# GNN layer with normalisation: 29 node ranges summed from one-hot products and 1610 nodes from row gathers, instead of 35 ranges and 650 nodes

## The chip, the cores and the metric

One core of one Trainium2 chip runs the kernel. The metric is device time of one execution in microseconds. The kernel before took 628.18 us (median of 3 runs, 627.49 to 630.49). Its five engines are TensorE (PE, with its weight loads shown apart as PEld), VectorE (DVE), ScalarE (ACT), GpSimd (POOL) and SyncE (SP); SP only issues transfers here.

## What is computed

There are 6250 nodes with 128 features, and 100,000 edges sorted by destination. An edge of type 0 carries its source's features times W_data plus b_data, an edge of type 1 those times W_control plus b_control. Messages are summed per destination; the node's own product is added, then ReLU, a residual and a layer norm.

```python
m_data = Xs @ W_data.T + b_data          # Xs = X[src]
m_ctrl = Xs @ W_control.T + b_control
msg = jnp.where((edge_types == 0)[:, None], m_data, m_ctrl)
agg = jax.ops.segment_sum(msg, dst, num_segments=X.shape[0])
out = jax.nn.relu(agg + (X @ W_self.T + b_self))
x = _layernorm(x + out, axis=-1)
```

## The kernel before, in words

**The message table.** L422 to L472 compute both products for every node, 128 nodes to a block, two blocks to a round q (25 rounds). Each float32 product is kept as three bfloat16 parts that add up to it (m3, 98 tiles of 128 rows and 384 columns). m3 stays in SBUF and is also written to DRAM as `table`, one transfer per round, on SP for even and on ACT for odd rounds (L470).

**Ranges (windows).** The first 5600 nodes are summed in 35 ranges of WN = 160 nodes, in groups of 1, 2 and eight times 4 ranges (GROUPS, L35). A range reads 2688 sorted edges. `ranks` (L582) works on a group at once. For each of 21 edge columns it builds a one-hot of the source tile (hots, L638), and PE counts with triangular weights how many earlier edges have the same tile (L648, accumulator rk). DVE takes the maximum (slot, L652). Each edge so gets one of 32 slots in its tile. One-hots of the slots (hr, L667; two, L673) scatter the edge's row and destination into those slots (L682). Edges that find no slot go to a list of 64 (hl, L749); their rows are fetched from `table` by a slot gather on POOL (sr, L790), whose index `at` comes from DVE (L778), and copied by SP to gl (L797). The slot table goes through DRAM (packed) and comes back broadcast to all partitions (rows, L832); DVE turns it into one-hots (L840).

`sums` (L823) then runs over the ranges. In each of 25 steps g, PE selects message rows with four matmuls of 32 output rows (L860), ACT or DVE copies the result out of PSUM (gs, L405 or L406), and PE adds it to the destination rows with one-hots hot2 built by DVE (L847): L874 for 128 of the range's nodes, L877 for the other 32.

**The last nodes.** The last 650 nodes are summed in six blocks of up to 128 (`gathered`, L892). A block takes nt columns of 128 edges (GT: 18 for a full block, 3 for the last; 93 in all). DVE works out each edge's table row and its destination code (eight operations of nt columns, L903 to L916). For each column POOL gathers 128 rows of `table` (L924, buffer t_msg, eight of them), DVE builds a one-hot (L929, buffer t_hot), and PE adds (L935) into the single accumulator ga.

**Closes.** `close` (L485) finishes a group of ranges or a block: ACT copies one third of the accumulator and DVE adds the other two (L520, L523), then residual and ReLU (L531), statistics (L535, L537), eight small operations, the scaling on ACT or DVE, and a store by SP (L574). The 32 remaining nodes of a group's ranges are gathered in one further block (f).

**The order of the work.** Every operation is given to `Plan` (L83) with an engine, a duration in us, a due time and what it reads and writes. `Plan.run` (L120) simulates the engines, picks the operation with the earliest due time among those that are ready, and emits the program in that order. Each engine then executes its own list strictly in order. The constants SEM (a hop between engines), OTHER and LAT are part of this model. `add` takes a buffer's ring length (bufs): a buffer is free for reuse when the users of the one that many places before it are through.

Ranges fall due at T0 + 13 us each, and gathers are spread over g0 = T0 + 2 TW to g1 = T0 + (NW - 2) TW (L965 to L970).

Of the kernel before, what the change touches and what calls it, by code (L numbers as in the profile page):

```python
# [33 lines left out]
WIN = KT * P  # L34
GROUPS = [1, 2] + [4] * 8  # L35
NW = sum(GROUPS)
# [7 lines left out]
NGB = -(-(N - NW * WN) // P)  # L44
GT = [-(-(min(P, N - NW * WN - P * i) * 17) // P) + 1 for i in range(NGB)]
NBD = -(-(NW + NGB) // 16) * 16

# [35 lines left out]
class Plan:  # L83
    SEM = 0.12
    OTHER = 0.5
# [34 lines left out]
    def run(self):  # L120
# [31 lines left out]
        while len(order) < n:  # L152
# [75 lines left out]
def act(cols):  # L228
    return 0.055 + cols / 1200

def sums_over_windows(ctx, tc, x, xt, edges, w, bias, out, total):
# [20 lines left out]
    TW = 13.0  # L252
    LAT = 0.15

# [124 lines left out]
    def load_edges(b, n, out_, due, buf, key, engine):  # L379
        def fn():  # L380
# [41 lines left out]
    for q in range(NS):  # L422
# [36 lines left out]
        for i in range(3 if q >= DQ else 0):  # L459
            d = due + 0.6 + 1.2 * i  # L460
            evict(lambda mv3=mv3, i=i: mv3(i), pv3, n, d, [mp], [(m3, (q, i))])
            if i < 2:
# [22 lines left out]
    def close(tag, n0, step, rows, sums_a, block, due):  # L485
# [12 lines left out]
        if block:  # L498
            xb = B(work, [D, len(block), W4], F32, "xb", 2, 4 * W4)
            for j, (at, _) in enumerate(block):  # L500
# [12 lines left out]
            add("PE", 0.6, mms, due, [xb, w_sb, one3, brows, fold] + [b for _, b in block], [f])  # L513
        mv = B(work, [P, nb, 2], F32, "mv" + tag, 2, 10)
        for k in range(nb):
            if k < nw:
                a, da = sums_a[k]
                m = m0
                s = B(work, [P, D], F32, "s", 3)
                add("ACT", act(D), lambda a=a, s=s, m=m: A.copy(s.t[:m], a.t[:m, 0:D]), da, [a],  # L520
                    [s])
                for c in (1, 2):
                    vec(da, D, lambda a=a, s=s, c=c, m=m: V.tensor_add(  # L523
                        s.t[:m], s.t[:m], a.t[:m, c * D : (c + 1) * D]), [a, s], [s])
# [6 lines left out]
            vec(da, D, lambda src=src, k=k, m=m: V.scalar_tensor_tensor(  # L531
                h.t[:m, k, :], src(), 0.0, xr.t[:m, k, :], op0=ALU.max, op1=ALU.add),
                [got] + [(xr, key) for key in keys], [(h, ("a", k))] + [(h, key) for key in keys])
            st = B(work, [P, 6], F32, "st", 4)
            add("DVE", 0.2, lambda k=k, st=st, m=m: V.bn_stats(st.t[:m], h.t[:m, k, :]), da + 1,  # L535
                [(h, ("a", k))], [st])
# [45 lines left out]
    def ranks(gi, w0, nw, when, step, engines):  # L582
# [308 lines left out]

    def gathered(bi, when, step):  # L892
        nt, n0 = GT[bi], NW * WN + bi * P
        nn = min(P, N - n0)
        gi = len(GROUPS) + bi
        top = max(GT)
        G2 = lambda name, dt=F32: B(work, [P, nt], dt, "t_" + name, 2, top)
        raw = B(work, [P, nt, 3], I32, "t_raw", 2, 3 * top)
        load_edges(NW + bi, nt * P, lambda: raw.t, when - 12, raw, None, "SP")
        rel, lows, ins, far, code = (G2(k) for k in ("rel", "lows", "ins", "far", "code"))  # L900
        cb, idx = G2("cb", I32), G2("idx", I32)
        d = when - 6
        vec(d, nt, lambda: V.tensor_scalar_add(rel.t, raw.t[:, :, 1], 1.0 - n0), [raw], [rel])  # L903
        vec(d, nt, lambda: V.tensor_single_scalar(lows.t, rel.t, nn + 0.5, op=ALU.is_lt), [rel],
            [lows])
        vec(d, nt, lambda: V.scalar_tensor_tensor(
            ins.t, rel.t, 0.5, lows.t, op0=ALU.is_ge, op1=ALU.mult,
            accum_out=counts.t[:, gi : gi + 1]), [rel, lows], [ins, (counts, gi)])
        vec(d, nt, lambda: V.tensor_single_scalar(cb.t, raw.t[:, :, 0], 7,
                                                  op=ALU.arith_shift_right), [raw], [cb])  # L910
        vec(d, nt, lambda: V.tensor_single_scalar(far.t, raw.t[:, :, 2], 0.0, op=ALU.not_equal),
            [raw], [far])
        vec(d, nt, lambda: V.tensor_add(far.t, far.t, cb.t), [far, cb], [far])
        vec(d, nt, lambda: V.scalar_tensor_tensor(
            idx.t, far.t, 128.0, raw.t[:, :, 0], op0=ALU.mult, op1=ALU.add), [far, raw], [idx])
        vec(d, nt, lambda: V.tensor_mul(code.t, rel.t, ins.t), [rel, ins], [code])  # L916
        xc = B(work, [D, P], F32, "t_xc", 2)
        add("SP", 0.1, lambda: S.dma_start(xc.t[:, :nn], xt[:, n0 : n0 + nn]), when, m3_key(6), [xc],
            lat=2.5)
        ga = B(ps, [P, 512], F32, "ga", 1)  # L920
        for k in range(nt):
            at = when + step * k
            m = B(work, [P, D3], BF16, "t_msg", 8)
            add("POOL", 1.25, lambda m=m, k=k: G.indirect_dma_start(  # L924
                out=m.t, out_offset=None, in_=table[:, :],
                in_offset=bass.IndirectOffsetOnAxis(ap=idx.t[:, k : k + 1], axis=0)),
                at, [idx, table_b], [m], lat=2.0)
            hot = B(work, [P, P], BF16, "t_hot", 4)
            vec(at + 2, P, lambda hot=hot, k=k: V.tensor_scalar(  # L929
                hot.t, iota1_b.t[:, :P], code.t[:, k : k + 1], None, op0=ALU.is_equal),  # L930
                [code, (iota1_b, 0)], [hot], 0.26)

            def mm(m=m, hot=hot, k=k):
                for j in range(-(-nn // R)):
                    T.matmul(ga.t[R * j : R * j + R, :D3], hot.t[:, R * j : R * j + R], m.t,  # L935
                             start=k == 0, stop=False, skip_group_check=True)
            add("PE", 0.165, mm, at + 4.5, [hot, m], [ga])
        end = when + step * nt + 6
        add("PE", 0.3, lambda: own(lambda j, m: ga.t[R * j : R * j + m, :D],
                                   lambda j, m: xc.t[:, R * j : R * j + m], nn), end,  # L940
            [xc, w_sb, one3, brows], [ga])
        close("g", n0, nn, nn, [(ga, end)], [], end + 2)

# [15 lines left out]
    for gi, w0, nw, *_ in todo:  # L959
# [4 lines left out]
              T0 + (w0 + nw) * TW + 2)  # L964
    total_tiles = sum(GT)  # L965
    g0, g1 = T0 + 2 * TW, T0 + (NW - 2) * TW
    done = 0
    for bi, nt in enumerate(GT):
        gathered(bi, g0 + (g1 - g0) * done / total_tiles, (g1 - g0) / max(total_tiles, 20))
        done += nt  # L970
    total_ps = low()
# [147 lines left out]
```

## Time and profile before

| quantity | value |
|---|---|
| median of 3 runs | 628.18 us |
| the profiled execution, its own time | 627.98 us |
| its span, first to last instruction | 626.0 us |
| mean granted TensorE clock | 0.960 |
| ACT copies of gs, L405 | 835, 353.9 us busy |
| PE selection, L860 | 3430 matmuls |
| gathers by POOL, L924 | 93 |
| slot gathers by POOL, L790 | 18 |
| mean DMA rate | 108 GB/s |

Busy times are unions of the records of an engine. Matmul and DVE records overlap their successors, so the sum of single durations is more than the busy time. The profile's list of groups gives the mean length of one record.

### The profile page before, as it was taken

What the parts mean: (1) busy time and instruction counts of PE and PEld (TensorE: products, weight loads), DVE (VectorE), ACT (ScalarE), POOL (GpSimd) and SP (SyncE); (2) the same over time, 40 slices, a digit from 0 to 9 for tenths busy, and PEclk for the clock granted to TensorE, in tenths of its full rate; (3) what the DMA queues carried; (4) which work ended last, traced back from release to release, by engine and by line L of the source; (5) the groups of instructions that cost most, each with busy time, mean ns of one, the idle gap of its engine ahead of it and who ended that gap; (6) DMA issues with size and microseconds to landing.
All of it is one profiled execution on the core that took longest, in us unless ns stands there. A gap on an engine that the chain in (4) does not pass through costs nothing.

```text
span 626.0 us, 31669 instructions
## 1 busy us (share of the span) xinstructions
PE 547.3 (87%) x13418; PEld 417.8 (67%) x13418; DVE 519.5 (83%) x1848; ACT 447.4 (71%) x1152; POOL 114.0 (18%) x119
## 2 busy tenths in 40 slices
PE   4987979979998899899889998999899899988890
PEld 3554646747776677777667876787677678766670
DVE  6966788999999899998999999899979888865512
ACT  3656656747687767877777788778678777887890
POOL 1000162030411054200134210163100342000000
PEclk9989897979999899999999999999999999998996
DMA  3889372062225313530344143225410442142000
GB/s 89 251 264 278 97 212 88 11 214 67 77 71 176 96 51 109 175 115 5 129 132 143 44 129 115 92 64 161 133 62 7 154 136 83 46 143 76 7 5 26
DMA packets 58585, 67.86 MB, mean 108 GB/s; under 512 B 19390, under 2 KB 49587, under 8 KB 58435
## 3 DMA queue, kind: packets, MB, share of 16 engines
q1 hardware_dynamic: 45585, 48.25, 24.7%
q0 software_dynamic: 5360, 10.98, 6.5%
q10 hardware_dynamic: 7490, 6.52, 3.2%
q8 instruction: 107, 1.75, 1.1%
q14 instruction: 43, 0.35, 0.2%
HBM read 50.73 MB, written 13.27 MB: 102 GB/s over the span
## 4 chain that ended last, share of the span: by engine, by line
DVE 53%; PE 31%; DMA 6%; ACT 4%; issue 3%; SPq 1%; ACTq 0%; DVEq 0%
DVE hot L847 10%; PE a L874 9%; PE g L860 9%; DVE slot L652 8%; PE rk L648 4%; DVE hots L638 4%; DVE two L673 4%; DVE rows L840 3%; ACT gs L405 3%; DVE s L523 3%; PE g L440 2%; DMA rows<-packed 2%; DVE st L535 2%; PE a L877 2%; DVE hr L667 2%
## 5 line engine op out<-in xcount | busy, mean ns | idle before, releaser
L405 ACT CAST gs<-g 128x384 bf16<-128x384 f32 x835 | 353.9, 481 | 98.1 <-PE g L860 90.8
L860 PE MATMUL g<-m,rows 128*32 128x384 bf16 x3430 | 321.0, 332 | 2.4 <-DVE rows L840 1.5
L874 PE MATMUL a<-gs,hot 128*32 128x384 bf16 x3360 | 309.5, 333 | 12.1 <-ACT gs L405 5.3
L860 PEld LDWEIGHTS <-rows 128*32 128x32 bf16 x3430 | 217.7, 135 | 15.1 <-DVE rows L840 2.6
L877 PE MATMUL a<-gs,hot 128*32 128x128 bf16 x2520 | 201.6, 221 | 0.1
L874 PEld LDWEIGHTS <-hot 128*32 128x32 bf16 x3500 | 153.7, 95 | 68.1 <-issue 33.2
L924 POOL DMA_INDIRECT t_msg<-table,t_idx x93 | 94.4, 1015 | 218.5 <-PE ga L935 166.9
L652 DVE TENSOR_REDUCE slot<-rk 128x4 f32<-128x392 f32 (+2 forms) x210 | 106.8, 509 | 17.6 <-PE rk L648 16.1
L847 DVE TENSOR_TENSOR hot<-iota_b,to_d 128x800 bf16<-128x800 bf16 x175 | 94.5, 567 | 25.7 <-PE a L877 20.3
L877 PEld LDWEIGHTS <-hot 128*32 128x32 bf16 x2625 | 98.1, 97 | 5.9 <-issue 0.6
L648 PE MATMUL rk<-hots,rest 128*32 128x392 bf16 (+2 forms) x800 | 74.9, 323 | 25.4 <-DVE slot L652 25.1
L648 PE MATMUL rk<-hots,tri 128*32 128x392 bf16 (+2 forms) x840 | 84.2, 319 | 7.4 <-DVE hots L638 7.4
L648 PEld LDWEIGHTS <-rest 128*32 128x32 bf16 x800 | 35.2, 97 | 48.0 <-issue 43.4
L638 DVE TENSOR_TENSOR hots<-iota_b,st 128x392 bf16<-128x392 bf16 (+2 forms) x210 | 60.5, 330 | 1.3 <-PE vt L682 1.1
L790 POOL DMA_INDIRECT sr<-table,at x18 | 17.0, 943 | 207.1 <-DVE at L778 140.3
L840 DVE TENSOR_SCALAR rows<-rows,pid 128x1568 bf16<-128x1568 bf16 x70 | 42.5, 627 | 4.6 <-DMA rows<-packed 4.5
L648 PEld LDWEIGHTS <-tri 128*32 128x32 bf16 x840 | 36.3, 98 | 11.2 <-DVE tri L312 6.7
L935 PE MATMUL ga<-t_msg,t_hot 128*32 128x384 bf16 x363 | 37.1, 327 | 3.3 <-DVE s L523 2.6
L440 PE MATMUL g<-w_sb,xc 128*128 128x256 f32 x98 | 34.1, 440 | 1.2 <-ACT m L405 0.6
L523 DVE TENSOR_TENSOR s<-s,a 128x128 f32<-128x128 f32 x70 | 19.8, 283 | 16.5 <-ACT s L520 15.4
L405 ACT CAST m<-g 128x512 bf16<-128x512 f32 (+1 forms) x43 | 23.3, 579 | 13.6 <-PE g L465 5.8
L682 PEld LDWEIGHTS <-two 128*64 128x64 bf16 x735 | 18.8, 109 | 15.0 <-DVE two L673 11.3
(173 smaller groups left out, 573.6 us busy)
## 6 DMA issues: line engine op xcount, KB each, us to landing
rows<-packed SPq DMA_DIRECT2D x35, 784.0 KB
table<-m SPq DMA_DIRECT2D x12, 384.0 KB
table<-m ACTq DMA_DIRECT2D x12, 384.0 KB
xc<-in_xt SPq DMA_DIRECT2D x8, 320.0 KB
xr<-in_x SPq DMA_DIRECT2D x8, 256.0 KB
out<-xr SPq DMA_DIRECT2D x8, 256.0 KB
gl<-sr SPq DMA_DIRECT2D x35, 48.0 KB
xc<-in_xt ACTq DMA_DIRECT2D x6, 256.0 KB
```

The lines of the kernel that those rows point to most:

```text
L405: [("ACT", act(cols), lambda: A.copy(o(), src())), ("DVE", dve(cols), lambda: V.tensor_copy(o(), src()))], None, None, due, r, w, lat)
L440: T.matmul(o, xa.t[:, at : at + P], w_sb.t[:, : 2 * D], start=i == 0, stop=False, skip_group_check=True)
L523: vec(da, D, lambda a=a, s=s, c=c, m=m: V.tensor_add(s.t[:m], s.t[:m], a.t[:m, c * D : (c + 1) * D]), [a, s], [s])
L638: vec(due - (2.0 if k else 0.5), nw * NT, lambda k=k, hot=hot, k0=k0: V.tensor_tensor(hot.t[:, k - k0].rearrange("p w (c d) -> p w c d", d=2),
L648: T.matmul(acc.t[R * j : R * j + R, : nw * NT], wt.t[:, R * j : R * j + R], m, start=start, stop=stop, skip_group_check=True)
L652: vec(due, nw * NT, lambda k=k: V.tensor_reduce(slot.t[:, k, :], acc.t[:, : nw * NT].rearrange("p (w c) -> p w c", c=NT), axis=AX.X, op=AL ...
L840: add("DVE", dve(half * NT, 0.26), lambda sp=sp, rs=rs: V.tensor_scalar(sp.t[:, rs], sp.t[:, rs], pid1.t, None, op0=ALU.is_equal), due - 4 ...
L847: V.tensor_tensor(hot2.t[:, c0 : c0 + 5].rearrange("p g (c d) -> p g c d", d=2), iota1_b.t.rearrange("p (c d) -> p c d", d=2)[:, None].to_ ...
L860: T.matmul(gp.t[R * t : R * t + R, :D3], sp.t[:, :, 4 * g + t], m3.t[:, 4 * g + t, :], start=True, stop=True)
L874: T.matmul(a.t[R * j : R * j + R, :D3], hot2.t[:, g, R * j : R * j + R], gs.t, start=g == 0, stop=False, skip_group_check=True)
L877: T.matmul(a.t[R * c : R * c + R, D3:], hot2.t[:, g, P:], gs.t[:, c * D : (c + 1) * D], start=False, stop=last, skip_group_check=True)
L924: add("POOL", 1.25, lambda m=m, k=k: G.indirect_dma_start(out=m.t, out_offset=None, in_=table[:, :], in_offset=bass.IndirectOffsetOnAxis(a ...
```

## The change

The ranges become 29 (groups of 1, 2, six times 4, and 2) and cover 4640 nodes. The last 1610 nodes go to 13 blocks: twelve of 18 columns and one of 11, 227 gathers.

`gathered` now takes up to four blocks at once: one set of the eight preparing operations for all of them, with the blocks' first nodes from gbase. The destination codes are kept in pairs of bfloat16. One DVE operation builds the one-hots of up to six columns (KB) by comparing two tensors. There are six message buffers instead of eight, two one-hot buffers of six columns instead of four of one.

Besides, in `close`, one reduce over the three thirds replaces ACT's copy and two adds; the remainder's xt loads become one transfer. Rounds q with q % 5 of 3 or 4 take their product accumulator from the ring "a" (two) instead of "g" (three). The table goes out in pairs of rounds, on SP alone; the loads of xt go on SP except chunk 1. The copies to to_d are for ACT only. The planner's hop depends on the engine, LAT is 0.1, and some durations are longer.

```diff
-GROUPS = [1, 2] + [4] * 8
+GROUPS = [1, 2] + [4] * 6 + [2]
+GB = 4
-    SEM = 0.12
+    HOP = {"PE": 0.22, "ACT": 0.15, "DVE": 0.11, "POOL": 0.12, "SP": 0.12}
-                    o.ready = max(o.ready, op.end + (0.0 if same else op.lat + self.SEM))
+                    o.ready = max(o.ready, op.end + (0.0 if same else op.lat + self.HOP[e]))
-    LAT = 0.15
+    LAT = 0.1
+    vec(2, 1, lambda: V.memset(counts.t, 0.0), [], [counts])
+    acopy = lambda o, src, cols, due, r, w: add(
+        "ACT", 0.1 + cols / 1000, lambda: A.copy(o(), src()), due, r, w)
-            e = ("ACT", A) if c % 2 else ("SP", S)
+            e = ("ACT", A) if c == 1 else ("SP", S)
-                xa.t, xt[:, c * CH * P : c * CH * P + n]), due - 4, [], [xa], lat=3.0)
+                xa.t, xt[:, c * CH * P : c * CH * P + n]), due - 5, [], [xa], lat=3.0)
-        mp = B(ps, [P, 512], F32, "g", 3)
+        mp = B(ps, [P, 512], F32, *(("a", 2) if q % 5 > 2 else ("g", 3)))
-        e = ("ACT", A) if q % 2 else ("SP", S)
-        add(e[0], 0.1, lambda ts=ts, e=e: e[1].dma_start(tv[:, ts, :], m3.t[:, ts, :]), due + 8,
-            m3_key(q), [(table_b, q)], lat=3.5)
+        if q % 2 or q == NS - 1:
+            t0 = 4 * (q - q % 2)
+            add("SP", 0.1, lambda t0=t0, t1=ts.stop: S.dma_start(
+                tv[:, t0:t1, :], m3.t[:, t0:t1, :]), due + 8, m3_key(q) + m3_key(q - q % 2),
+                [(table_b, q)], lat=4.5)
-                add("SP", 0.1, lambda at=at, j=j: S.dma_start(
-                    xb.t[:, j, :], xt[:, at : at + R]), due - 20, late, [(xb, j)], lat=2.5)
+            add("SP", 0.1, lambda: S.dma_start(
+                xb.t, xt[:, b0:b1_].rearrange("d (b p) -> d b p", p=WN)[:, :, P:]), due - 20, late,
+                [xb], lat=2.5)
-                add("ACT", act(D), lambda a=a, s=s, m=m: A.copy(s.t[:m], a.t[:m, 0:D]), da, [a],
-                    [s])
-                for c in (1, 2):
-                    vec(da, D, lambda a=a, s=s, c=c, m=m: V.tensor_add(
-                        s.t[:m], s.t[:m], a.t[:m, c * D : (c + 1) * D]), [a, s], [s])
+                vec(da, D3 + 70, lambda a=a, s=s, m=m: V.tensor_reduce(
+                    s.t[:m], a.t[:m, :D3].rearrange("p (c d) -> p d c", c=3), axis=AX.X,
+                    op=ALU.add), [a], [s])
-                copy(lambda t=t, par=par, nx=nx: to_d.t[R * t : R * t + R, par : nw : 2, :nx, :],
+                acopy(lambda t=t, par=par, nx=nx: to_d.t[R * t : R * t + R, par : nw : 2, :nx, :],
+    gbase = C([P, NGB], I32, "gbase")
+    add("POOL", 0.2, lambda: G.iota(gbase.t, pattern=[[P, NGB]], base=NW * WN - 1,
+                                    channel_multiplier=0), 3, w=[gbase])
+    def gathered(bis, when, step):
+        nt, k_ = GT[bis[0]], len(bis)
+        n = nt * k_
+        raw = B(work, [P, k_, nt, 3], I32, "t_raw", 2, 3 * top)
+        for j, bi in enumerate(bis):
+            load_edges(NW + bi, nt * P, lambda j=j: raw.t[:, j], when - 14 + 0.1 * j, raw, j, "SP")
+        G2 = lambda name, dt=F32: B(work, [P, k_, nt], dt, "t_" + name, 1, top)
+        cb, idx = G2("cb", I32), B(work, [P, n], I32, "t_idx", 2, top)
+        code = B(work, [P, n, 2], BF16, "t_code", 2, 2 * top)
...
+        vec(d, 2 * n, lambda: V.tensor_tensor(code.t, f2(rel), f2(ins), op=ALU.mult), [rel, ins],
+            [code])
+        KB = 6
+        for j, bi in enumerate(bis):
...
+            start = when + step * nt * j
...
+            ga = B(ps, [P, 512], F32, "ga", 1)
+            for k in range(nt):
+                at = start + step * k
+                kk = j * nt + k
+                if k % KB == 0:
+                    kn = min(KB, nt - k)
+                    hot = B(work, [P, kn, P], BF16, "t_hot", 2, KB * P)
+                    s4 = [P, kn, P // 2, 2]
+                    vec(at + 1, kn * P, lambda hot=hot, kk=kk, kn=kn, s4=s4: V.tensor_tensor(
+                        hot.t.rearrange("p k (c d) -> p k c d", d=2),
+                        iota1_b.t[:, :P].rearrange("p (c d) -> p c d", d=2)[:, None]
+                        .to_broadcast(s4), code.t[:, kk : kk + kn, None, :].to_broadcast(s4),
+                        op=ALU.is_equal), [code, (iota1_b, 0)], [hot], 0.52)
+                m = B(work, [P, D3], BF16, "t_msg", 6)
+                add("POOL", 1.25, lambda m=m, kk=kk: G.indirect_dma_start(
+                    out=m.t, out_offset=None, in_=table[:, :],
+                    in_offset=bass.IndirectOffsetOnAxis(ap=idx.t[:, kk : kk + 1], axis=0)),
+                    at, [idx, table_b], [m], lat=2.0)
...
+            close("g", n0, nn, nn, [(ga, end)], [], end + 2)
+    step = max((g1 - g0) / max(sum(GT), 20), 1.3)
+    full = len(GT) - (GT[-1] != GT[0])
+    for b0 in range(0, NGB, GB):
+        for bis in (range(b0, min(b0 + GB, full)), range(max(b0, full), min(b0 + GB, NGB))):
+            if len(bis):
+                gathered(list(bis), g0 + step * done, step)
```

More of the change, by code (lines that the diff above doesn't have):

```diff
@@ L499, in close @@
             xb = B(work, [D, len(block), W4], F32, "xb", 2, 4 * W4)
+            b0, b1_ = block[0][0] - P, block[-1][0] + R
             for j, (at, _) in enumerate(block):
@@ L530, in close @@
                 got, src = f, lambda f=f, m=m: f.t[:m, :D]
-            vec(da, D, lambda src=src, k=k, m=m: V.scalar_tensor_tensor(
+            vec(da, D + 70, lambda src=src, k=k, m=m: V.scalar_tensor_tensor(
                 h.t[:m, k, :], src(), 0.0, xr.t[:m, k, :], op0=ALU.max, op1=ALU.add),
@@ L534, in close @@
             st = B(work, [P, 6], F32, "st", 4)
-            add("DVE", 0.2, lambda k=k, st=st, m=m: V.bn_stats(st.t[:m], h.t[:m, k, :]), da + 1,
+            add("DVE", 0.28, lambda k=k, st=st, m=m: V.bn_stats(st.t[:m], h.t[:m, k, :]), da + 1,
                 [(h, ("a", k))], [st])
@@ L889, in sums @@
         return got
[L892 to L904, printed above, removed]
+    gbase = C([P, NGB], I32, "gbase")
@@ new lines, in sums_over_windows @@
+    add("POOL", 0.2, lambda: G.iota(gbase.t, pattern=[[P, NGB]], base=NW * WN - 1,
[3 more added lines that the diff above has]
+        n = nt * k_
+        gi = len(GROUPS) + bis[0]
+        top = GB * max(GT)
+        raw = B(work, [P, k_, nt, 3], I32, "t_raw", 2, 3 * top)
+        for j, bi in enumerate(bis):
+            load_edges(NW + bi, nt * P, lambda j=j: raw.t[:, j], when - 14 + 0.1 * j, raw, j, "SP")
+        G2 = lambda name, dt=F32: B(work, [P, k_, nt], dt, "t_" + name, 1, top)
+        rel, lows, ins, far = (G2(k) for k in ("rel", "lows", "ins", "far"))
+        cb, idx = G2("cb", I32), B(work, [P, n], I32, "t_idx", 2, top)
+        code = B(work, [P, n, 2], BF16, "t_code", 2, 2 * top)
+        d = when - 8
+        nn = min(P, N - NW * WN - P * bis[0])
+        fl = lambda b: b.t.rearrange("p b k -> p (b k)")
+        f2 = lambda b: fl(b)[:, :, None].to_broadcast([P, n, 2])
+        vec(d, n, lambda: V.tensor_sub(
+            rel.t, raw.t[:, :, :, 1], gbase.t[:, bis[0] : bis[0] + k_, None].to_broadcast(
+                [P, k_, nt])), [raw, gbase], [rel])
+        vec(d, n, lambda: V.tensor_single_scalar(lows.t, rel.t, nn + 0.5, op=ALU.is_lt), [rel],
@@ L905, in gathered @@
             [lows])
-        vec(d, nt, lambda: V.scalar_tensor_tensor(
+        vec(d, n, lambda: V.scalar_tensor_tensor(
             ins.t, rel.t, 0.5, lows.t, op0=ALU.is_ge, op1=ALU.mult,
             accum_out=counts.t[:, gi : gi + 1]), [rel, lows], [ins, (counts, gi)])
[L909 to L942, printed above, removed]
+        vec(d, n, lambda: V.tensor_single_scalar(cb.t, raw.t[:, :, :, 0], 7,
+                                                 op=ALU.arith_shift_right), [raw], [cb])
+        vec(d, n, lambda: V.tensor_single_scalar(far.t, raw.t[:, :, :, 2], 0.0,
+                                                 op=ALU.not_equal), [raw], [far])
@@ new lines, in gathered, with mm @@
+        vec(d, n, lambda: V.tensor_add(far.t, far.t, cb.t), [far, cb], [far])
+        vec(d, n, lambda: V.scalar_tensor_tensor(
+            idx.t.rearrange("p (b k) -> p b k", k=nt), far.t, 128.0, raw.t[:, :, :, 0],
+            op0=ALU.mult, op1=ALU.add), [far, raw], [idx])
+        vec(d, 2 * n, lambda: V.tensor_tensor(code.t, f2(rel), f2(ins), op=ALU.mult), [rel, ins],
+            [code])
+        KB = 6
+        for j, bi in enumerate(bis):
+            n0 = NW * WN + bi * P
+            xc = B(work, [D, P], F32, "t_xc", 2)
+            start = when + step * nt * j
+            add("SP", 0.1, lambda xc=xc, n0=n0: S.dma_start(xc.t[:, :nn], xt[:, n0 : n0 + nn]),
+                start, m3_key(6), [xc], lat=2.5)
+            ga = B(ps, [P, 512], F32, "ga", 1)
[16 more added lines that the diff above has]
+                    at, [idx, table_b], [m], lat=2.0)
+                def mm(m=m, hot=hot, k=k, ga=ga):
+                    for i in range(-(-nn // R)):
+                        T.matmul(ga.t[R * i : R * i + R, :D3], hot.t[:, k % KB, R * i : R * i + R],
+                                 m.t, start=k == 0, stop=False, skip_group_check=True)
+                add("PE", 0.165, mm, at + 4.5, [hot, m], [ga])
+            end = start + step * nt + 6
+            add("PE", 0.3, lambda ga=ga, xc=xc: own(
+                lambda i, m: ga.t[R * i : R * i + m, :D],
+                lambda i, m: xc.t[:, R * i : R * i + m], nn), end, [xc, w_sb, one3, brows], [ga])
+            close("g", n0, nn, nn, [(ga, end)], [], end + 2)
@@ L964, in sums_over_windows @@
               T0 + (w0 + nw) * TW + 2)
-    total_tiles = sum(GT)
     g0, g1 = T0 + 2 * TW, T0 + (NW - 2) * TW
+    step = max((g1 - g0) / max(sum(GT), 20), 1.3)
     done = 0
-    for bi, nt in enumerate(GT):
-        gathered(bi, g0 + (g1 - g0) * done / total_tiles, (g1 - g0) / max(total_tiles, 20))
-        done += nt
+    full = len(GT) - (GT[-1] != GT[0])
[3 more added lines that the diff above has]
+                gathered(list(bis), g0 + step * done, step)
+                done += sum(GT[bi] for bi in bis)
     total_ps = low()
```

## The prediction, made before the result was known

> **What bounds the kernel now.** I read the busy shares first, then stretches of 60 us in the steady part, then the pace of TensorE (PE) where it runs alone, then GpSimd (POOL), whose work the change grows most. The page's first part:
>
> ```profile
> PE 547.3 (87%) x13418; PEld 417.8 (67%) x13418; DVE 519.5 (83%) x1848; ACT 447.4 (71%) x1152; POOL 114.0 (18%) x119
> ```
>
> PE and VectorE (DVE) share the work; POOL is idle four fifths of the time. Two stretches, each as long as one group of four ranges (columns: stretch, length, busy of PE, PEld, DVE, ACT, POOL, granted clock, DMA share, GB/s):
>
> ```profile
> 247.00:307.00 60.00, 54.91 (x1496) 43.88 (x1500) 55.18 (x188) 46.14 (x120) 5.70 (x6) 1.00 0.31 95
> 307.00:367.00 60.00, 55.18 (x1496) 44.15 (x1488) 56.01 (x192) 46.00 (x121) 19.65 (x20) 1.00 0.37 114
> ```
>
> Both engines are 92 to 93% busy, so neither has slack: a group costs about 60 us because it needs 55 us on each of two coupled engines. The second stretch holds 18 gathers' matmuls (72 by the tile ga), the first 4 (16), and the time is the same within what the stretches show. The list step L749, once per group, starts at 130.96, 184.99, 246.87, 305.20, 366.67, 426.32, 484.54 and 543.8: periods of 54 to 62 us. After the last, PE and ACT work off about six ranges until 609 us, and the last close and store take 17 us more. The pace of PE alone, from the timeline near the end (start, length):
>
> ```profile
> 554.77 0.35 PE L874 MATMUL a<-gs,hot 128*32 128x384 bf16 x4
> 554.93 0.24 PE L877 MATMUL a<-gs,hot 128*32 128x128 bf16 x3
> 554.96 0.38 PE L860 MATMUL g<-m,rows 128*32 128x384 bf16 x4
> 555.16 0.35 PE L874 MATMUL a<-gs,hot 128*32 128x384 bf16 x4
> ```
>
> One step of a range (L860, L874, L877) repeats every 0.39 us, though the records last 0.35 each: they overlap. Four matmuls of 384 columns are 1536 of the step's 3456 columns, 0.173 us. A row's mean is therefore not its cost; the spacing is. POOL:
>
> ```profile
> 82.24 0.95 POOL L924 DMA_INDIRECT t_msg<-table,t_idx  x1 [0.30 <-issue]
> 83.49 0.94 POOL L924 DMA_INDIRECT t_msg<-table,t_idx  x1 [0.30 <-issue]
> ...
> L924 POOL DMA_INDIRECT t_msg<-table,t_idx x93: 940/946/1753, 77.2 to 521.1; - x93
> ...
> POOL t_msg L924 <- PE ga L935: 166.9, 39, 31.7
> POOL sr L790 <- DVE at L778: 140.3, 9, 39.3
> ```
>
> Gathers follow each other every 1.25 us when nothing holds them (mean busy 1.015 + 0.30 = 1.31). POOL otherwise waits for free message buffers or, in order, for the slot gather sr.
>
> **Part by part: PE.** One range of 160 nodes costs 25 steps x 0.39 + 0.28 (own product, L479 and L482 at 551.64) = 10.0 us. A four-range group adds its rank passes: 41 passes of 392 columns x 0.177 = 7.2, the slot scatter 2.6 (L682 in 307 to 367), prefix and lists 0.9, its remainder block 0.5: 11.2 us. Two such groups go: 2 x (40.0 + 11.2) = 102.4. One two-range group comes: 20.0 + 41 x 0.09 (spacing at 196 columns near 62.5 us) + 1.3 + 0.9 + 0.3 = 26.2. Added: 134 gathers x 0.173 = 23.2, and 7 own products of closes x 0.28 = 2.0. Net -51.0 us of PE. At the 92% of the stretches, -55: span 626.0 - 55 = 571.
>
> **DVE.** In 307 to 367, with each line's own busy time: L847 10.98, L840 4.94, L652 11.49, L638 6.49, L667 2.00, L673 3.70, L523 2.84, L929 4.01. Of the 56.0 I take off L929 and one gathered close with its preparation (about 4) and have 48 us for a four-range group. Two go (-96). The two-range group: L638 21 x 0.19, L652 21 x 0.27, one-hots of slots 3.3, L847 and L840 8.0, closes 2.5, small operations about 7: +30.5. Seven more gathered closes, each one reduce 0.55, L531 0.22, L535 0.22, L537 0.11, eight small ones at 0.15, one scale 0.2 = 2.5: +17.5. The gather one-hots: 93 x 0.22 (4.01/18) = 20.7 become 38 of up to 768 columns at the 0.52 of the nearest row (L673 at 768, 0.552 less overlap): 19.7, -1. Preparation: six times 1.32 (43.18 to 44.50) becomes four times about 1.7, -1. The to_d copies on DVE (37 x 0.15) move to ScalarE (ACT), -6. Net -56; over 0.925, -61: span 565.
>
> **One reduce for a copy and two adds.** Nearest row: L652, 392 columns out of PSUM, 0.559, against 2 x 0.283 for L523. Taken as nothing; the strided read is not in the trace, and at half rate it would be 42 x 0.41 = +17 us, which I keep for the range. ACT loses 42 copies of 0.27.
>
> **ACT** loses 150 evictions at 0.42 (five in 2.1 near 75 us), 63 us, against 37 copies x 0.27 = 10 gained: it stays off the bound.
>
> **A third sum, by periods.** L749 of the first four-range group stays at 131. Then five periods: the first 54 to 58, four with about 33 gathers instead of 6 to 20. Periods with 20 gathers issued took 62, those with 6 took 58 and 59: 0.25 us per gather, so about 65. That gives 131 + 58 + 260 = 449. The two-range group's period: 2.5 ranges worked off meanwhile, 37, to 486. Then 5.5 ranges remain (six less 2.5, plus two): 56, some last gathers 3, the end 17: 562. The three sums say 571, 565, 562; I take 566. Around the span lie 627.98 - 626.0 = 2.0 us, hence 568; the profiled execution is 0.2 below the median of 628.18, which I leave.
>
> **POOL.** 227 gathers and 15 slot gathers (18 less the two for each of two groups, plus one) x 1.31 = 317 us, between 76 us (L790 and the first gather, when the table is complete) and about 525: 70% of it. It is covered while six message buffers (eight before) are enough: PE takes one each 1.9 us (430/227), so six cover 11.4 us. The Trainium skill speaks against this part: "SBUF — State Buffer", section "A bandwidth-pool intuition that's wrong (but worth ruling out)", says that a DMA whose descriptors GpSimd writes took about 3.1 us instead of 0.62 beside a VectorE copy holding the port they share. By the rule 242 x 3.1 = 750 us, more than the span. The row decides: median 946 and longest 1753 ns with DVE 92% busy, so 317 us.
>
> Landing: the chain of waits has
>
> ```profile
> 188.04 5.09 DMA sr<-table,at
> ```
>
> while "DMA: Bandwidth & Descriptors", section "Anatomy of one DMA — SWDGE (gpsimd) path", fits 2.0 us plus bytes over 436 GB/s, 2.2 us for 98 KB, about what the planner books. By the fit a buffer is held 2.2 us before PE can use it, by the row 5.1 (the gather's 0.95 within it); I take the row, leaving 11.4 - 5.1 = 6 us of cover.
>
> **Queues and waits that move.** SP takes all table writes (13 instead of 25 in all) and five more loads of xt; it drops 3 issues per block (0.42 each) and gains 7 edge loads (0.83) and three issues for each of 7 closes (0.5), about 16 us over 450. The closes' stores wait on SP for DVE; behind them stand loads of rows, which are issued 12 planned us ahead. Cover gone, each costs up to 2 us: 14. In the head the table writes now wait on one queue behind and ahead of range loads; SP waited there 14.5 us for ACT's m, and DVE 4.3 for rows. Five banks for the products instead of three work against that. Together -6 to +8; taken 0, since the end of the table is set by 25 rounds on ACT. The new durations in the planner only reorder; the idle of PE, 4.7 in 60, bounds a gain at about 25 us, and I allow as much loss; taken 0. The memset and the iota (0.15) lie before 2 us.
>
> **Rivals.** *Dry buffers at the slot gathers:* POOL stops at sr until DVE has at; the gathers behind it are stuck, and PE stands before a message with its ranges queued behind. For it: 140.3 us in nine waits. Against: those stood where no gather was due. Price: eight groups' waits, each one landing less one step, 5.1 - 1.9 = 3.2 us, 26 us: about 594. *Slower:* turnaround of the six buffers becomes the bound. PE frees a buffer late because its fixed order puts other work between, POOL refills late, PE waits. It decides when one turn of six exceeds 6 x (626 - 76 - 30)/227 = 13.7 us; at 15 us (2.5 each) 76 + 568 + 30 + 2 = 676. Against it: ten gathers passed in 13 us from 411 to 424, though with eight buffers. *The better order:* half of PE's idle goes, about 552.
>
> **How the numbers follow.** The sums hold 0.58 (556 to 580), dry buffers 0.20 (580 to 610), better order 0.09 (544 to 556), slower 0.11, and 0.02 lands within 0.5%, about what a measurement of this kernel can tell from no change, by both losses at once. Faster 0.87, same 0.02, slower 0.11. The range 546 to 606 leaves out the slow rival, some of the far ends, about 2 in 10.
>
> **What would show it.** Right: PE about 496 and DVE about 463 us busy, POOL 240 to 250; nothing or little under PE waiting for t_msg; L749 periods of 63 to 67; spacing 1.25 at L924. Wrong: PE waiting for DMA t_msg for more than 20 us; L924 busy over 1.5 us; the strided reduce near 1 us; the table complete after 82 us.

## The result and the profile after

The kernel after takes 548.13 us (median of 4 runs, 547.09 to 550.25) beside 627.84 us for the kernel before (4 runs, 626.32 to 630.49): a ratio of 0.873, with a 95% interval of 0.869 to 0.877. The forecast was 568 us, with a range of 546 to 606: the time lies in it, near its lower end. 80 us went where 60 were forecast. Lines move by a few: L860 is now L866, L874 L880, L877 L883, L652 L658, L749 L755, L790 L796, L924 L958, L935 L965, L929 L952.

The page's first part, for the kernel after (span 546.8 us, own time 548.72 us):

```profile
PE 483.3 (88%) x11972; PEld 380.5 (70%) x11972; DVE 463.3 (85%) x1615; ACT 387.0 (71%) x981; POOL 252.2 (46%) x251
```

DVE lost 56 us of busy time and PE 64, and POOL's more than doubled. Two stretches of one four-range group each (columns as before):

```profile
249.00:313.00 64.00, 59.15 (x1614) 48.05 (x1606) 60.61 (x201) 47.42 (x122) 38.61 (x39) 1.00 0.49 141
313.00:375.00 62.00, 58.49 (x1597) 48.85 (x1592) 58.18 (x183) 48.07 (x126) 38.37 (x39) 1.00 0.49 144
```

A group now carries 36 gathers and takes 62 to 64 us. PE and DVE are 92 to 95% busy in it: the same two engines bound the kernel, a little more tightly than before. The waits (engine, tile and line, releaser: us in total, times, longest; dots stand for rows left out):

```profile
POOL t_msg L958 <- PE ga L965: 93.6, 78, 21.8
...
POOL t_msg L958 <- PE g L866: 41.0, 68, 2.4
...
POOL sr L796 <- DVE at L784: 13.9, 7, 7.2
...
PE rk L654 <- DVE slot L658: 8.4, 17, 1.3
...
PE a L880 <- ACT gs L407: 5.5, 10, 1.2
```

POOL waits for PE to free message buffers. For the slot gathers' index it waits hardly any more (13.9 us against 140.3; one wait of 65.8 us in the head, before the table is complete, stays as it was, 64.4 before). PE has no wait for t_msg at all. The tile t_msg, and two of the by-form groups of VectorE (busy, mean ns | idle before):

```profile
L958 POOL DMA_INDIRECT t_msg<-table,t_idx x227: 940/947/2712, 78.8 to 505.3; - x114
```

```profile
L952 DVE TENSOR_TENSOR t_hot<-iota_b,t_code 128x768 bf16<-128x768 bf16 x37 | 20.5, 553 | 1.4 <-PE ga L965 1.3
L528 DVE TENSOR_REDUCE s<-a 128x128 f32<-128x384 f32 x29 | 16.0, 553 | 24.8 <-ACT bs L407 15.2
```

A gather occupies POOL for 0.947 us in the median (0.946 before), the first starts at 78.8 us instead of 77.2, and the one reduce takes 0.553 us, about as much as the two adds of 0.283 that it replaces; ACT's copy falls away besides.

### The profile page after: what moved, and what is told of

It reads as the page before. It is cut to its first block, busy times and chain, and to the rows that moved or that the text cites. A ratio compares the mean times of both kernels' runs of the same rounds, so it can differ in the third digit from the quotient of the medians.

```text
span 546.8 us, 28398 instructions
## 1 busy us (share of the span) xinstructions
PE 483.3 (88%) x11972; PEld 380.5 (70%) x11972; DVE 463.3 (85%) x1615; ACT 387.0 (71%) x981; POOL 252.2 (46%) x251
## 4 chain that ended last, share of the span: by engine, by line
## 5 line engine op out<-in xcount | busy, mean ns | idle before, releaser
L407 ACT CAST gs<-g 128x384 bf16<-128x384 f32 x684 | 293.2, 480 | 89.5 <-PE g L866 81.3
L958 POOL DMA_INDIRECT t_msg<-table,t_idx x227 | 235.1, 1036 | 163.5 <-PE ga L965 93.6
L866 PE MATMUL g<-m,rows 128*32 128x384 bf16 x2842 | 272.3, 332 | 1.7 <-DVE rows L846 1.4
L880 PE MATMUL a<-gs,hot 128*32 128x384 bf16 x2784 | 264.2, 331 | 9.4 <-ACT gs L407 5.5
L866 PEld LDWEIGHTS <-rows 128*32 128x32 bf16 x2842 | 177.2, 135 | 17.3 <-DVE rows L846 2.8
L883 PE MATMUL a<-gs,hot 128*32 128x128 bf16 x2088 | 167.2, 220 | 1.1 <-issue 1.1
L880 PEld LDWEIGHTS <-hot 128*32 128x32 bf16 x2900 | 124.0, 96 | 36.5 <-issue 17.0
L658 DVE TENSOR_REDUCE slot<-rk 128x4 f32<-128x392 f32 (+2 forms) x189 | 90.4, 478 | 24.3 <-PE rk L654 19.8
L965 PE MATMUL ga<-t_msg,t_hot 128*32 128x384 bf16 x897 | 91.5, 331 | 2.3 <-DVE s L528 2.3
L883 PEld LDWEIGHTS <-hot 128*32 128x32 bf16 x2175 | 83.9, 97 | 7.1 <-issue 2.7
L853 DVE TENSOR_TENSOR hot<-iota_b,to_d 128x800 bf16<-128x800 bf16 x145 | 76.6, 565 | 0.0
L796 POOL DMA_INDIRECT sr<-table,at x15 | 14.4, 957 | 81.8 <-DVE t_far L931 65.8
L965 PEld LDWEIGHTS <-t_hot 128*32 128x32 bf16 x897 | 41.9, 98 | 6.7 <-issue 3.6
```

Of the source, the lines that this page charges most:

```text
L407: [("ACT", act(cols), lambda: A.copy(o(), src())), ("DVE", dve(cols), lambda: V.tensor_copy(o(), src()))], None, None, due, r, w, lat)
L658: vec(due, nw * NT, lambda k=k: V.tensor_reduce(slot.t[:, k, :], acc.t[:, : nw * NT].rearrange("p (w c) -> p w c", c=NT), axis=AX.X, op=AL ...
L853: V.tensor_tensor(hot2.t[:, c0 : c0 + 5].rearrange("p g (c d) -> p g c d", d=2), iota1_b.t.rearrange("p (c d) -> p c d", d=2)[:, None].to_ ...
L866: T.matmul(gp.t[R * t : R * t + R, :D3], sp.t[:, :, 4 * g + t], m3.t[:, 4 * g + t, :], start=True, stop=True)
L880: T.matmul(a.t[R * j : R * j + R, :D3], hot2.t[:, g, R * j : R * j + R], gs.t, start=g == 0, stop=False, skip_group_check=True)
L883: T.matmul(a.t[R * c : R * c + R, D3:], hot2.t[:, g, P:], gs.t[:, c * D : (c + 1) * D], start=False, stop=last, skip_group_check=True)
```

## The experiments

Three theories stood against each other. **Work:** the time falls because work leaves PE and DVE (the expectations call it theory A), most of it with the ranges, and the other edits save some DVE time. **Order:** the planner's new constants make a better order, and much of the gain is theirs. **Buffers:** gathers held back by the six message buffers set the periods. Each edit below makes `Plan` order the program anew, so no experiment keeps the order as it was.

Chips differ here, and without that the numbers can't be read. On the chips of most runs the kernel before takes 627 to 629 us. Seven runs were made on two other chips, where it took 682 and 684 us, and the ratios there are others. They stand apart below. Each chip was used at one time only, so what is put down to the chip may belong to that time.

**Both kernels once more.** No edit.

> The kernel after, unchanged, on the chip of the experiments, as their base. If the chip stretches both kernels alike: 0.873 of the kernel before, about 595 us where that takes 682. If what is slower there (crossings of engines) hits the gathers more: above 620 us, and then the experiments with 35 and with 29 ranges are to be compared with it and not with 548.

> The kernel before, unchanged, with a profile on the chip of the experiments, where it took 682 us in the runs beside them and not 628. If every matmul is slower there, the last two ranges, where TensorE runs alone, step slower than 0.39 us; if only crossings between engines or transfers are slower, that pace is 0.39 and the four-range periods are longer than 60 us.

Both ran on a chip where the kernel before takes 626.92 us, so they don't answer what the two texts ask of the chips with 682 us. Measured: 549.43 us (ratio 0.873, 0.867 to 0.880), and the kernel before, run once more, 628.49 us. The result came again as it was.

**All but the ranges.** The kernel after with the old ranges (93 gathers):

```diff
-GROUPS = [1, 2] + [4] * 6 + [2]
+GROUPS = [1, 2] + [4] * 8
```

> All edits of the change except the split (35 ranges, 93 gathers), again, to be compared on a chip where the kernel before takes 627 us and the one after 549. Theory A, the split carries the gain and the other edits make its gathers cheap for VectorE: VectorE falls by 25 us, TensorE by nothing, and TensorE binds: 610 to 628 us. Rival B, the other edits carry a good part by themselves: 600 or less. Where the kernel before took 682, this one took 0.983 of it, which would be 616 here.

Measured: 614.27 us, ratio 0.980 (0.975 to 0.986). The page's first part:

```profile
PE 535.0 (87%) x13418; PEld 421.3 (69%) x13418; DVE 507.5 (83%) x1681; ACT 447.3 (73%) x1134; POOL 117.5 (19%) x120
```

The other edits alone are worth 14 us, as the work theory expected (610 to 628 us) and against the 600 or less of its rival. DVE does 12 us less, where 25 were expected. PE runs the same 13418 matmuls and shows 12 us less busy time too, which is a warning: the ends of its records are modelled, and their union is not a fixed sum of work.

**The ranges alone.** The kernel before with the new ranges:

```diff
-GROUPS = [1, 2] + [4] * 8
+GROUPS = [1, 2] + [4] * 6 + [2]
```

> The kernel before with 29 ranges and nothing else, again on such a chip. Theory A, both engines bind: VectorE falls by only 13 us (one-hots column by column, 13 preparations), so 605 to 618 us. If TensorE alone sets the time: about 570. Where the kernel before took 682, this one took 1.011 of it, which would be 634 here: then crossings or the order of the work, and not the sums of the engines, decide.

Measured: 581.86 us, ratio 0.927 (0.922 to 0.931): 47 us less than the 628.56 of that chip. That lies outside the 605 to 618 us that the work theory expected, and closer to the 570 expected if PE alone set the time. Its page's first part, and two of its waits:

```profile
PE 488.8 (84%) x11972; PEld 374.7 (65%) x11972; DVE 491.7 (85%) x1947; ACT 387.4 (67%) x1002; POOL 250.0 (43%) x250
```

```profile
PE rk L648 <- DVE slot L652: 31.3, 38, 4.3
...
PE ga L935 <- DVE s L523: 10.1, 9, 2.7
```

DVE has 28 us less to do than before, not 13 less, but 28 more than in the kernel after, and PE waits for it: 31.3 us for slots, against 25.1 before and 8.4 after.

Alone the two parts give 0.980 and 0.927, whose product is 0.908; together they give 0.873. Some 20 us belong to neither alone. The steady stretches, each from the start of a list step to the start of another, show where they come from. The kernel before, six groups with 72 gathers:

```profile
185.00:543.80 358.80, 331.87 (x8940) 264.95 (x8933) 327.27 (x1110) 276.14 (x722) 79.65 (x79) 1.00 0.34 103
```

All but the ranges, six groups with 72 gathers:

```profile
183.30:531.60 348.30, 324.87 (x8934) 270.43 (x8932) 317.15 (x979) 277.29 (x713) 85.23 (x81) 1.00 0.36 107
```

The ranges alone, four groups with 144 gathers:

```profile
186.20:465.60 279.40, 241.79 (x6419) 193.16 (x6419) 256.85 (x992) 190.28 (x504) 156.03 (x153) 0.99 0.45 128
```

The kernel after, four groups with 144 gathers:

```profile
186.00:437.00 251.00, 234.62 (x6414) 194.21 (x6414) 236.74 (x769) 189.44 (x487) 158.27 (x154) 1.00 0.49 143
```

Divided by the number of groups:

| kernel | gathers in a period | its period, us | PE busy | DVE busy |
|---|---|---|---|---|
| before | 12 | 59.8 | 55.3 | 54.5 |
| all but the ranges | 12 | 58.1 | 54.1 | 52.9 |
| the ranges alone | 36 | 69.9 | 60.4 | 64.2 |
| after | 36 | 62.8 | 58.7 | 59.2 |

With the old code 24 more gathers lengthen a period by 10.1 us, 0.42 each, DVE's busy time by 0.40 and PE's by 0.21. With the new code they lengthen it by 4.7 us, 0.20 each, DVE's by 0.26 and PE's by 0.19. A gather here has its share of its block's preparation and close with it. The one-hots of the gathers in one period of each, the ranges alone (L929) and the kernel after (L952), columns: stretch, length, busy of DVE, granted clock, DMA share, GB/s:

```profile
256.00:325.00 69.00, 8.37 (x36) 1.00 0.46 131
```

```profile
249.00:313.00 64.00, 3.32 (x6) 1.00 0.49 141
```

36 single ones occupy 8.37 us and six of six columns 3.32, 0.14 us less for each gather. By as much, 0.14 us for each gather, the other edits shorten DVE's busy time in a period, with 12 gathers (54.5 to 52.9) and with 36 (64.2 to 59.2). The whole times agree: these edits took off 14 us with 93 gathers and 34 with 227 (581.86 to 548.13), 0.15 us a gather in both. So what they gain grows with the number of gathers, which is the interaction. That it is the blocks of one-hots that do it rests on this count alone: DVE's other savings, the common preparation and the copies to to_d, ran with them, more copies of gs on DVE ran against them, and the blocks were not taken back alone on such a chip.

**The old constants of the planner.** The kernel after with

```diff
-    HOP = {"PE": 0.22, "ACT": 0.15, "DVE": 0.11, "POOL": 0.12, "SP": 0.12}
+    HOP = {"PE": 0.12, "ACT": 0.12, "DVE": 0.12, "POOL": 0.12, "SP": 0.12}
-    LAT = 0.1
+    LAT = 0.15
```

> The kernel after with the planner's hop 0.12 for every engine and LAT 0.15, again on such a chip. Theory A, they only reorder at no gain: 549 within 5. Rival: the longer booked hop behind TensorE keeps each copy of gs and each matmul that reads it further apart in the order, so that a wait is filled; with the old constants 570 us or more, and TensorE waits for ACT gs longer than the 5.5 us of the kernel after. Where the kernel before took 682, this one took 1.004 of it.

Measured: 550.78 us (549.41 to 551.61), ratio 0.877 (0.873 to 0.881). Two of its waits:

```profile
PE rk L654 <- DVE slot L658: 12.8, 14, 5.1
...
PE a L880 <- ACT gs L407: 8.8, 14, 1.5
```

PE stands some 8 us longer in these two (21.6 against 13.9), and the time is 1 to 3 us longer than the two measurements of the kernel after (549.43 and 548.13), too little to be told from no change. The rival's 570 or more didn't come. HOP and LAT explain next to nothing of the 80 us: the order theory falls as far as these constants go. The longer durations of single operations in the planner weren't undone.

**On the chips where the kernel before takes 682 and 684 us.** The first three are the edits above; the next three change the kernel after:

```diff
-                m = B(work, [P, D3], BF16, "t_msg", 6)
+                m = B(work, [P, D3], BF16, "t_msg", 3)
```

(e4_msg3, and again x_msg3),

```diff
-        KB = 6
+        KB = 1
-                    hot = B(work, [P, kn, P], BF16, "t_hot", 2, KB * P)
+                    hot = B(work, [P, kn, P], BF16, "t_hot", 4, KB * P)
```

(x_kb1), and 27 ranges with 273 gathers:

```diff
-GROUPS = [1, 2] + [4] * 6 + [2]
+GROUPS = [1, 2] + [4] * 6
```

(x_27).

> All edits of the change except the split: 35 ranges and six gathered blocks (93 gathers) as before. Theory A (the working of the prediction: the split does it, the other edits only make the gathers cheap for VectorE): VectorE loses 12 us of one-hots (93 x 0.22 to 0.09), about 5 of preparation and 8 of copies, 25 in all; TensorE loses nothing and binds, so 615 to 628 us. Rival B (the other edits carry a good part by themselves, through order, accumulator banks and transfers): 600 us or less.

> The kernel before with 29 ranges and nothing else: 227 gathers with one-hots built column by column and 13 separate preparations. Theory A, both engines bind: TensorE falls by 51 us or more, but VectorE has 134 x 0.22 = 29 us of one-hots more than in the kernel after, 8 of preparation, 6 of copies, so it falls only by about 13 us: 605 to 618 us, VectorE over 92% busy until the last list step. If TensorE alone sets the time: about 570. If the POOL queue with in-order slot gathers were the bound without the new order: over 628.

> The kernel after with the planner's hop 0.12 for every engine and LAT 0.15 as before; the durations given to close's operations stay new. If the new hops bring the 20 us by which the prediction was short: about 568. Theory A (they only reorder, taken as nothing in the prediction): 548 within 5.

> The kernel after with three message buffers instead of six. By the prediction's turnaround: a buffer is held about 5.1 us from issue to landing plus its wait for TensorE; three buffers at one gather each 1.9 us cover 5.7 us, so nearly every late message shows: 560 to 590, and TensorE waiting for t_msg. If landing takes 2 to 3 us when the queues are free, three are enough: within 5 us of 548.

> The kernel after with one-hots of the gathers built one column at a time (KB = 1, four buffers), all else as after. Theory C (VectorE's relief is what the split needs: 29 ranges alone took 582 us with VectorE 492 us busy, the whole change 549 with 463): VectorE works 16 to 29 us more (227 x 0.16 to 0.22 against 20), and the time rises by 10 to 25 us, to 560 to 575. Rival (the other edits of order and banks make the difference): within 5 us of 549.

> The kernel after with 27 ranges and 1930 nodes in 16 blocks: 273 gathers and 14 slot gathers, 287 x 1.31 = 376 us of GpSimd. If TensorE and VectorE still set the time: two ranges and one two-range group less (26.2 and 30.5 us) for 46 gathers and three closes (9 and about 13 us): about 17 us less, 528 to 536. If GpSimd begins to bind (376 us out of 77 to about 490): 549 or more, with TensorE waiting for t_msg.

> The kernel after with three message buffers instead of six, on the same chip as the two others. By the prediction's turnaround (5.1 us held before TensorE can use a message, one gather each 1.9 us): three cover 5.7 us, so late messages show, 555 to 590, with TensorE waiting for DMA t_msg. If the wait is hidden by the order: 549 within 5.

| kernel | us there | ratio there, interval | us where before takes 627 to 629 |
|---|---|---|---|
| all but the ranges (e1_35_rest) | 668.78 | 0.983, 0.977 to 0.989 | 614.27 |
| the ranges alone (e2_29_only) | 688.61 | 1.011, 1.003 to 1.019 | 581.86 |
| old constants (e3_old_plan) | 684.42 | 1.004, 1.001 to 1.008 | 550.78 |
| three buffers (e4_msg3) | 647.56 | 0.952, 0.946 to 0.958 | not run |
| three buffers (x_msg3) | 653.55 | 0.957, 0.949 to 0.966 | not run |
| one column a time (x_kb1) | 691.42 | 1.012, 1.005 to 1.019 | not run |
| 27 ranges (x_27) | 717.57 | 1.050, 1.043 to 1.057 | not run |

The edits that gain 47 and 78 us elsewhere gain nothing there; only the edits without new ranges keep their 2%. The kernel after itself was not run on these chips; the nearest base is e3_old_plan, 1 to 3 us from it elsewhere. Against that base, one column at a time costs about 1%, 5 us, hardly clear of the intervals, while DVE's busy time rises by 18 us (from 470.5 to 488.3): DVE, 71% busy, was not the limit there. 27 ranges cost 5%, where 17 us less were expected. Half the buffers gain 5%, where the buffer theory has fewer of them cost time, though PE does wait for t_msg then, 10.1 and 8.6 us. These runs say nothing sure about other chips: what block one-hots, further gathers and fewer buffers are worth where the kernel before takes 627 us was not measured one by one and stays open. Of the buffers only the profile after speaks: PE never stood before a message.

## Why the prediction came out as it did, step by step

**The bound.** PE and DVE as two coupled engines without slack: right. In the steady stretches they are 92 to 95% busy after the change too, and the time followed them; POOL, with 138 us more, set no end. The forecast of the time was 20 us too long all the same: 60 us less were forecast and 80 came, and the time lies where the forecast put a chance of 0.09.

**DVE's sum.** 519.5 - 56 = 463 was forecast, 463.3 measured, in part by luck: in the time that each operation adds to DVE's busy union, those that write to_d took off 9 us where 6 were taken, and seven more copies of gs on DVE put 3 back. The one reduce at no cost was the right choice of its two bounds (0.553 us; half rate, by the forecast's estimate of 0.41 more, would have been about 0.96).

**PE's sum.** 496 was forecast, 483.3 measured. The ranges alone came to 488.8, and the other edits took the rest. The gathers are not what is missing: within one code each raised PE's busy time by 0.21 us (old) and 0.19 (new), more than the 0.173 taken. The 13 us were not split up further; since all but the ranges moved the busy time of unchanged matmuls by 12 us, they need not be work at all.

**The third sum, term by term.** It said 562 us of span; 546.8 came. Its terms against the starts of the list step L755 (133.35, 185.92, 249.35, 312.95, 375.26, 436.88, 494.81):

| term | forecast | measured |
|---|---|---|
| start of the first four-range group's list step | 131 | 133.3 |
| the first period | 58 | 52.6 |
| four periods with gathers | 4 x 65 = 260 | 251.0 |
| the two-range group's period | 37 | 57.9 |
| what is left after it | 76 | 52.0 |
| sum | 562 | 546.8 |

The four periods and the first one are 9 and 5 us shorter than forecast. The step "0.25 us per gather", read from two kinds of period of the kernel before, is the price of neither program: with the old code a gather costs 0.42 us, with the new one 0.20, and the other edits shorten even a period of 12 gathers by 1.7 us. The step took one price over from the old program, though the sum for DVE beside it had already made the one-hots cheaper. That 65 us is no farther off is luck: it lies between the 69.9 of the old code and the 62.8 of the new.

The last two terms are wrong one by one. In its period of 57.9 us PE worked off four ranges (395 matmuls of L866, 98 to a range) where 2.5 were taken, and three were left instead of 5.5 (294 of L866). The six ranges that the forecast counted behind the last list step of the kernel before were five (492 matmuls of L860). The sums of the two terms, 113 forecast and 110 measured, agree because most of the work moved from one into the other, and in part by luck.

**The idle time.** The first two sums took a fixed share of idle time with the work, 92% and 92.5% busy as before, and the new order as nothing. DVE's sum was right, yet it gave 565 us, because DVE's idle time fell too, from 106.5 us to 83.5, and PE's from 78.7 to 63.5. This is the term that both sums missed. Neither part of the change does that for PE by itself: PE's idle time is 76.5 us in all but the ranges and 91.3 in the ranges alone. One piece of it is the wait for DVE's slots, before and in all but the ranges:

```profile
PE rk L648 <- DVE slot L652: 25.1, 33, 3.9
```

```profile
PE rk L654 <- DVE slot L658: 9.7, 20, 1.0
```

It is 8.4 us after and 31.3 in the ranges alone, so this piece comes with the other edits. In the steady stretches PE's share is 93.5% (58.65 in 62.75). The time so fell into the span of the rival "better order" (544 to 556), but not for its reason: it has half of PE's idle go, 15 of 79 us went, and the constants of the planner gave 1 to 3 us. That the rest is the relief of DVE is likely and was not separated from the other edits; the planner's new durations weren't taken back in any run.

**POOL and the rule on the shared port.** The row was the right one: 947 ns in the median with DVE 92 to 95% busy, the longest 2.7 us, against the 3.1 us that the Trainium skill's page "SBUF — State Buffer", section "A bandwidth-pool intuition that's wrong (but worth ruling out)", gives for a transfer beside a VectorE copy. That figure is for a copy; which of VectorE's operations in this kernel hold the port no run shows, so the page is not refuted, only its use as a price for every gather here. POOL's 252.2 us were forecast as 240 to 250.

**The rivals.** Dry buffers: no, PE has no wait for t_msg, and sr waits for its index 13.9 us in all. Slower: in neither measurement of the kernel after; the turn of six buffers is (505.3 - 78.8)/226 x 6 = 11.3 us, under the 13.7 us from which that rival decides. (The ten gathers that the forecast counted from 411 to 424 us are eight in the trace.) Queues and waits that move, taken as nothing: the first gather starts 1.6 us later and the first four-range group 2.4 us later; what SP's new transfers, the product banks and the copies to to_d each do was only run together (14 us of gain with the reduce and the blocks).

## What to carry to other kernels

Where two coupled engines are full, price an added item on both, in the code that it will run in: here a gather, with its share of preparation and close, cost 0.42 us of a period in the old code, where its one-hot was one DVE operation, and 0.20 in the new, where six shared one. An edit that makes an item cheaper is worth the more the more items there are: the same edits gave 14 us with 93 gathers and 34 with 227, so try it together with the edit that adds them before dropping either. And measure on more than one chip, with the kernel before beside each: the same program (the old constants) gained 12% on one and nothing on another.

## What the runs showed of the hardware that was not expected

The kernel after with the old constants took 550.78 us on one chip and 684.42 us on another. Its single records are nearly as long there, and the mean granted clock is 0.941 against 0.960; if all of the time went with it, that would be 2%, not 24. Groups of the run on the second chip, then of the one on the first (busy, mean ns | idle before, releasers):

```profile
L407 ACT CAST gs<-g 128x384 bf16<-128x384 f32 x685 | 297.9, 481 | 208.4 <-PE g L866 109.4 <-PE ga L965 43.4 <-remote 28.2
L866 PE MATMUL g<-m,rows 128*32 128x384 bf16 x2842 | 280.1, 340 | 8.4 <-issue 6.6 <-DVE rows L846 1.5
L880 PE MATMUL a<-gs,hot 128*32 128x384 bf16 x2784 | 264.9, 340 | 65.7 <-ACT gs L407 50.7 <-issue 12.1 <-DVE gs L408 0.3
```

```profile
L407 ACT CAST gs<-g 128x384 bf16<-128x384 f32 x685 | 293.1, 480 | 87.2 <-PE g L866 78.3 <-PE rk L654 3.3 <-PE ga L965 1.3
L866 PE MATMUL g<-m,rows 128*32 128x384 bf16 x2842 | 269.7, 332 | 1.5 <-DVE rows L846 1.5
L880 PE MATMUL a<-gs,hot 128*32 128x384 bf16 x2784 | 260.2, 332 | 10.8 <-ACT gs L407 8.8 <-DVE gs L408 0.5 <-issue 0.4
```

The copy out of PSUM lasts 481 and 480 ns, a matmul's record 340 and 332. In the last ranges, where PE runs alone, a step takes 0.38 us on both (656.44 to 656.82 and 523.05 to 523.43, starts of L880), so not every matmul is slower. But ACT idles 208 us before its copies instead of 87, and PE 66 us before the adds instead of 11. The timeline of the second chip's run shows one such place:

```profile
312.13 0.41 PE L866 MATMUL g<-m,rows 128*32 128x384 bf16 x4
...
313.77 0.86 ACT L407 CAST gs<-g 128x384 bf16<-128x384 f32 x2 [1.91 <-PE g L866]
314.13 1.36 POOL L958 DMA_INDIRECT t_msg<-table,t_idx  x1 [1.23 <-PE g L866]
314.30 0.35 PE L880 MATMUL a<-gs,hot 128*32 128x384 bf16 x4 [1.76 <-ACT gs L407]
```

The last matmul that both wait for ended at about 312.54. ACT starts 1.23 us later, and everything behind it moves. Of ACT's copies of gs that waited over 0.25 us, 55 of 202 started more than 0.3 us after the last record of PE had ended on the second chip, and none of 131 on the first. The other runs agree: where the kernel before takes 627 to 629 us, none of 122 in the kernel after, of 120 in all but the ranges and of 124 in the ranges alone; where it takes 682 us, 28 of 149 in all but the ranges and 66 of 212 in the ranges alone. ACT itself is not late: the semaphore event that frees it comes 0.43 us (median) after PE's record in these 55, 0.02 in the others, and ACT starts 0.08 us after the event in both. Whether the event is late, or PE's work ended later than its modelled record says, the traces don't tell.

Of the 134 us between the two spans 111 are lost in the dense middle, from the first four-range list step to the last list step (473.2 against 361.8 us), 19 before it and 4 behind it. One period on the second chip:

```profile
298.00:381.00 83.00, 68.06 (x1616) 50.21 (x1616) 60.63 (x194) 48.44 (x124) 39.93 (x39) 0.98 0.38 110
```

83 us for a group that takes 62 to 64 us elsewhere, with about the same DVE (60.6 us) and a granted clock of 0.98. The loss is greater where there are more gathers: from one kind of chip to the other the kernels with 93 gathers take 1.09 times as long (614 to 669, and 627 to 682), those with 227 gathers 1.18 (582 to 689) and 1.24 (551 to 684), and three message buffers give 5% back. The kernels with 1.18 and 1.24 have the same number of gathers, so this number is not all of it. At the end of PE's record before a late start, packets of the gathers' DMA queue (q0) were in flight in 44% of the cases, and before the other waits in 29%; in the ranges alone on that chip it was 45 and 16%, in all but the ranges 39 and 7%. So late starts go with gathers under way, but more than half come without one. Why they come, and why on some chips, stays open.
